# A first row map for the first two slots of a mixture of experts, and the whole map behind it

## The chip, the core and the metric

One core of a Trainium2 chip runs the whole program. The metric is device time in microseconds; of the kernel before there are three runs, 1336.71, 1337.16 and 1341.0, median 1337.16. Engines are named as the profile names them: PE is TensorE (PEld its weight loads), DVE VectorE, ACT ScalarE, POOL GpSimd, SP the engine that issues most DMAs.

## The reference, cut to what matters

The model adds four blocks to x (4 x 512 tokens, 256 features): a mixture of experts, a block-wise linear attention, a conditioned attention and a two-layer feed-forward stack with local attention. The change lies in the mixture of experts alone:

```python
gate = xn @ wg_W + wg_b + (genre_embed @ gg_W + gg_b)
gate_w = jax.nn.softmax(gate, axis=-1)
topk_w, topk_i = jax.lax.top_k(gate_w, 2)                 # 2 of 8 experts for each token
h1 = jax.nn.relu(jnp.einsum('bsh,ehm->bsem', x, W1) + b1) # 256 -> 512
h2 = jax.nn.relu(jnp.einsum('bsem,emn->bsen', h1, W2) + b2) # 512 -> 512
out_e = jnp.einsum('bsen,enh->bseh', h2, W3) + b3         # 512 -> 256
return jnp.einsum('bseh,bse->bsh', out_e, cw)
```

Only the two chosen experts count for a token, so the kernel sorts the 4096 (token, choice) pairs by expert and computes each pair once.

## The kernel before, in words

*Routing* (lines 1215 to 1445). TensorE transposes x and computes the gate logits; DVE finds the two best experts of each token (`eqs`); TensorE counts, with triangular matrices, how many earlier tokens chose the same expert (`ppos`, `pcnt`); some fifty short DVE instructions make of it a place in a list of expert slots (`slots`, 1391). `SLOTS` (41) is the order in which slots are worked: a first one of 128 places, then seven of 256, and so on. `eid` (1409) names the expert of each slot; it hangs only on the counts.

*The row map* (1412 to 1445). The kernel needs the inverse: which token stands at a place. A place number is split into its high part (place // 64) and low part (place % 64), `hl` (1399). For each group of four token tiles, DVE makes a one-hot of the low parts (`ol`, 1417: 64 columns for each of two choices) and of the high parts (`oh`, 1422: NHI = 80 columns); the low one is multiplied by the token number, for choice 0 by four ACT instructions (1426), for choice 1 by one of DVE (1427). TensorE sums the product of both over all 16 tiles in `pmap` (choice 0 in partitions 0 to 63, choice 1 in 64 to 127; 32 matmuls). `hmap` (1434) copies it, a matmul with `mfold` adds the halves (`pmap2`), and DVE makes `rowtok` (1439, 1440), the token to gather for each place, and `goal` (1442, 1445), the row to scatter its result to. Then `busy(4)` (1455) queues four matmuls of 128 x 512 whose result nobody reads.

*The slots* (1662 to 1726). `loads(j, d)` (1468) reads the slot's expert from `eid` into a register of SP and issues its weights: `w1` 516 KB, `w2` 1024 KB, `w3` 640 KB, two buffers of each. `fetch(j, d)` (1486) gathers the slot's tokens, 128 rows of 1 KB each, by an indirect DMA on POOL from `rowtok`. `turn_tokens` (1493) transposes them (`pxb`), and ACT copies them to `xbT`. `layer` makes `h1` and `h2` with `relu` (1457), whose instructions alternate between ACT and DVE; `last` makes the output rows, and `scatter` writes them. In the first slot the order on TensorE is: `pxb` of slot 0, first layer (8 matmuls), `pxb` of slot 1, second layer (16 matmuls), first layer of slot 1.

*What sets the order.* A scheduler orders each engine's queue, except what is `pinned` or lies in `PE.in_order()`, which keeps its place as written. Each engine works through its queue in order.

## Time and profile before

| | |
|---|---|
| median of three runs | 1337.16 us |
| the profiled execution's own time | 1343.32 us |
| its span, first to last instruction | 1341.6 us |
| mean granted TensorE clock | 0.983 |
| busy: PE, DVE, ACT, POOL | 95%, 51%, 43%, 22% |
| slots of the mixture of experts | about 46 to 290 us |

The profile is one execution. A row of a group or of the timeline gives start or count, engine, source line, operation and tiles, and in brackets what ended the idle time before it. `PEclk` is the share of the full clock that TensorE was granted. Most matmuls stand under line 82, a helper's line, so they are told apart by their tiles (`pmap`, `pxb`, `ph`). A matmul of this type shows as two records. Ends of matmuls are modelled.

### The profile page before, as it was taken

The page shows a single profiled execution, that of the slowest core. Times are in us where ns is not written, and L with a number is a line of the kernel's source. Part 1 is how long each engine was busy: PE and PEld are TensorE (multiplying, and loading weights), DVE is VectorE, ACT ScalarE, POOL GpSimd, SP SyncE. Part 2 cuts the span into 40 slices and gives each one's busy share as a digit, 9 for nine tenths or more (in the row PEclk, how much of TensorE's full clock was granted, in tenths as well). Part 3 has the DMA queues.
Part 4 walks back from the last instruction along what each step waited for, and adds up shares of the span by engine and source line. Part 5 has one row for each costly group of instructions (what it writes and reads, how often), then busy time and mean ns, then how long its engine had stood idle before and what let it go on. Part 6 is the DMA issues. An engine that isn't in the chain of part 4 may idle for free.

```text
span 1341.6 us, 23073 instructions
## 1 busy us (share of the span) xinstructions
PE 1271.8 (95%) x9214; PEld 812.2 (61%) x9214; DVE 683.4 (51%) x1464; ACT 581.4 (43%) x1157; POOL 292.9 (22%) x321
## 2 busy tenths in 40 slices
PE   4899999998999999999999999999999998999998
PEld 3788899964566634344344655766555556667654
DVE  6221243425777733242237788654372877864421
ACT  3221233326655365646644646561222655463111
POOL 1322356420000101010103334210030333422010
PEclk7899999998999999999999999999999999999999
DMA  3565666523000000000210001311001011012000
GB/s 96 213 236 192 236 239 221 189 76 116 1 1 1 1 1 1 0 1 1 91 57 14 18 18 27 104 34 25 24 0 43 25 30 30 18 43 56 18 21 22
DMA packets 41856, 85.29 MB, mean 64 GB/s; under 512 B 9409, under 2 KB 25673, under 8 KB 39433
## 3 DMA queue, kind: packets, MB, share of 16 engines
q1 hardware_dynamic: 36600, 73.02, 16.9%
q0 software_dynamic: 3504, 9.46, 2.1%
q8 instruction: 77, 1.26, 0.4%
q10 hardware_dynamic: 1632, 1.21, 0.3%
q14 instruction: 43, 0.34, 0.1%
HBM read 74.76 MB, written 6.82 MB: 61 GB/s over the span
## 4 chain that ended last, share of the span: by engine, by line
PE 75%; DVE 9%; DMA 6%; ACT 5%; issue 3%; POOL 1%; SPq 0%; DVEq 0%; POOLq 0%
PE ph L82 11%; PE pdq L82 7%; PE pfy L82 6%; PE sc L82 6%; PE pua L82 5%; PE pug L82 5%; PE pv L82 5%; PE pdy L82 4%; PE po L82 3%; PE pn L82 3%; DMA ys<-ob,goal 2%; PE pds L82 2%; PE pqk L82 1%; PE pz L82 1%; PE pqt L86 1%
## 5 line engine op out<-in xcount | busy, mean ns | idle before, releaser
L82 PE MATMUL pdq<-wqkv,yT 128*128 128x512 f32 x384 | 171.7, 597 | 2.4 <-DVE t L626 2.2
L424 ACT ACTIVATE cex<-sc 128x512 f32<-128x512 f32 x256 | 132.2, 604 | 85.6 <-PE sc L82 84.6
L82 PEld LDWEIGHTS pdq<-wqkv,yT 128*128 128x128 f32 x384 | 71.1, 190 | 84.6 <-issue 76.1
L82 PE MATMUL ph<-h,w 128*128 128x256 f32 (+2 forms) x576 | 121.5, 370 | 0.3 <-ACT h L1596 0.3
L629 POOL TENSOR_TENSOR qr<-t,t 128x512 f32<-128x512 f32 x64 | 81.3, 1271 | 140.5 <-DVE t L626 140.5
L82 PEld LDWEIGHTS ph<-h,w 128*128 128x128 f32 x576 | 102.0, 192 | 15.2 <-ACT h L1596 0.5
L1461 DVE TENSOR_SCALAR h<-ph,w 128x256 f32<-128x256 f32 (+2 forms) x52 | 23.0, 461 | 121.8 <-PE ph L82 101.7
L394 POOL TENSOR_SCALAR fterm<-vw,faT 128x256 f32<-128x256 f32 x16 | 14.6, 920 | 317.6 <-DVE cr L384 317.6
L82 PE MATMUL sc<-qm,kT 32*128 32x512 f32 x512 | 82.6, 639 | 0.0
L681 ACT ACTIVATE p<-pds,ss 128x192 f32<-128x192 f32 (+1 forms) x256 | 79.8, 425 | 2.1 <-PE pds L82 0.8
L82 PE MATMUL pua<-hT,w 128*128 128x512 f32 x160 | 75.3, 593 | 0.9 <-DVE z L706 0.9
L82 PE MATMUL pug<-hT,w 128*128 128x512 f32 x160 | 76.2, 598 | 0.0
L619 ACT ACTIVATE sq<-pdq 128x512 f32<-128x512 f32 x64 | 38.5, 601 | 83.7 <-POOL qr L629 42.2
L714 POOL TENSOR_TENSOR p<-p 128x192 f32<-128x192 f32 x64 | 42.4, 682 | 138.1 <-PE pn L82 135.3
L796 ACT ACTIVATE gl<-pug,cols 128x512 f32<-128x512 f32 x40 | 27.3, 687 | 93.6 <-PE pug L82 90.8
L82 PE MATMUL pv<-cex,v 128*32 128x512 f32 x512 | 61.9, 598 | 2.7 <-DVE vw L391 2.7
L82 PE MATMUL pfy<-w,uA 128*128 128x256 f32 x256 | 61.4, 383 | 0.0
L82 PE MATMUL po<-w,h 128*128 128x256 f32 x264 | 60.1, 380 | 0.0
L82 PE MATMUL pdy<-wo,oT 128*128 128x256 f32 x256 | 58.9, 383 | 0.0
L684 DVE TENSOR_TENSOR p<-p,lmask 128x384 f32<-128x384 f32 x64 | 47.0, 735 | 23.0 <-ACT p L681 21.6
L82 PE MATMUL pn<-p,v 64*64 64x128 f32 (+1 forms) x1792 | 50.3, 254 | 8.2 <-DVE p L687 4.2
L1459 ACT ACTIVATE h<-ph,w 128x256 f32<-128x256 f32 (+2 forms) x52 | 22.4, 455 | 81.9 <-PE ph L82 78.0
(352 smaller groups left out, 2329.8 us busy)
## 6 DMA issues: line engine op xcount, KB each, us to landing
w<-in_moe_w_dram SPq DMA_DIRECT2D x18, 1024.0 KB, 7.9
w<-in_moe_w_dram SPq DMA_DIRECT2D x18, 516.0 KB, 4.0
w<-in_moe_w_dram SPq DMA_DIRECT2D x14, 640.0 KB, 4.5
zb<-rows SPq DMA_DIRECT2D x32, 256.0 KB, 4.1
g<-ys SPq DMA_DIRECT2D x6, 512.0 KB, 6.9
wqkv<-in_f_wqkv_dram SPq DMA_DIRECT2D x2, 1536.0 KB
w<-in_f_w_dram SPq DMA_DIRECT2D x2, 1408.0 KB
w<-in_moe_w_dram SPq DMA_DIRECT2D x4, 512.0 KB
```

The costliest lines, as they stand in the source:

```text
L82: cls._queue(nc.tensor.matmul(*args, **kw))
L86: cls._queue(nc.tensor.transpose(*args, **kw))
L394: nc.gpsimd.tensor_scalar_mul(fterm[:, t, :], vw, W["faT"][:, t, b : b + 1])
L424: nc.scalar.activation(ex[:, i, :], pss[2 * j + i], AF.Exp, scale=CHD**-0.5)
L619: nc.scalar.activation(sq, p3, AF.Square)
L629: nc.gpsimd.tensor_tensor(qr_t[:, s], t1, t2, ALU.add)
L681: nc.scalar.activation(p[:, j * 192 : j * 192 + n], pss[j // 2][r][:, j % 2 * 192 : j % 2 * 192 + n], AF.Exp, scale=d.ss[:, j, 1, 2 * c + ...
L684: nc.vector.tensor_tensor(edges, edges, lmask[:, :128].rearrange("p (s q) -> p s q", q=64).unsqueeze(1).to_broadcast([128, 3, 2, 64]), ALU ...
L714: nc.gpsimd.tensor_tensor(p[:, 1:, 0:64], p[:, 1:, 0:64], p[:, : NT - 1, 128:], ALU.add)
L796: nc.scalar.activation(gl, pg, AF.Gelu, bias=col("bg", l * (NU + 1) + i))
L1459: pinned(nc.scalar.activation(dst, src, AF.Relu, bias=bias))
L1461: pinned(nc.vector.tensor_scalar(dst, src, bias, 0.0, ALU.add, ALU.max))
```

## The change

It makes two row maps in place of one. The first has only the three columns of places that the first two slots need (`first`: one of slot 0, two of slot 1). Its one-hots of the high parts are six columns wide, and they are multiplied by the token numbers instead of the low parts; the one-hots of the low parts are made in three long instructions for all 16 tiles and lie in buffers of the output (`ols`). A filler `busy(12)` is queued in front of it. The gathers of the first two slots read `early_rows`.

The whole map follows: `oh` by groups of four tiles, the low one-hots scaled in place, products of groups 0 to 2 with fillers `busy(2)` and `busy(1)` among them, the transposes of slot 0, and the products of group 3. Its copy precedes slot 0's first ReLU on DVE; its fold, `rowtok` and `goal` come behind slot 0's first layer. `busy(4)` is gone. Slots behind the first read their expert from `eids`, which has the values of `eid` and is computed from `early_rows` too, so that it is not there before it. In slot 0's second layer the transposes for slot 1 stand ahead of the last block of four matmuls; they stood ahead of the whole layer.

```diff
             PE.matmul(ppos[:, :128], tot, mtiles[:, :128], start=False, stop=True)
+            busy(12)
...
+            first = [2 * NPAIR + SLOTS[0][0], 2 * SLOTS[1][0], 2 * SLOTS[1][0] + 1]
+            oh0 = y[2].rearrange("p t h -> p (t h)")[:, : 12 * B * NT].rearrange("p (k i n) -> p k i n", k=2, n=6)
+            for at, r, n in ((0, first[0], 2), (2, first[1], 4)):
+                one_hot(oh0[:, :, :, at : at + n], hl[:, 0], miota[:, 2 * r : 2 * r + n])
+            tokens = mtok.rearrange("p (k i) -> p k i", k=2)
+            pinned(nc.vector.tensor_tensor(
+                oh0, oh0, tokens.unsqueeze(3).to_broadcast([128, 2, B * NT, 6]), ALU.mult))
+            ols = [y[k].rearrange("p t h -> p (t h)").rearrange("p (i n) -> p i n", n=64) for k in (1, 3)]
+            one_hot(ols[0], hl[:, 1, 0], miota[:, :64])
+            for i0 in (0, B * NT // 2):
+                one_hot(ols[1][:, i0 : i0 + B * NT // 2], hl[:, 1, 1, i0 : i0 + B * NT // 2], miota[:, :64])
...
+            def map_products(pmap, n, onehot, k, tiles):
+                for i in tiles:
+                    PE.matmul(pmap[64 * k : 64 * k + 64, : 2 * n], ols[k][:, i, :], onehot(k, i),
+                              start=(i == 0), stop=(i == B * NT - 1))
...
+            with PE.in_order():
+                pmap = acct("pmap")
+                for k in range(2):
+                    map_products(pmap, 3, lambda k, i: oh0[:, k, i, :], k, range(B * NT))
+                early_rows = map_rows(map_copied(pmap, 3), 3)[1]
+            xbs = [hp.tile([128, 2, H], F32, tag="xb", name="xb", bufs=3) for j in range(2)]
+            gather(xbs[0][:, 0, :], early_rows, 0)
+            for i in range(2):
+                gather(xbs[1][:, i, :], early_rows, 1 + i)
...
+            eids = xp.tile([128, 1], I32, tag="eids", name="eids")
+            pinned(nc.vector.scalar_tensor_tensor(eids, early_rows[:, 0:1], 0.0, eid, ALU.min, ALU.max))
...
+            for g in range(4):
+                full_onehots(g)
+            busy(2)
+            for g in range(3):
+                full_products(g)
+                if g == 0:
+                    busy(1)
...
-                e = nc.sync.value_load(eid[j : j + 1, 0:1], min_val=0, max_val=NE - 1)
+                e = nc.sync.value_load((eids if j else eid)[j : j + 1, 0:1], min_val=0, max_val=NE - 1)
...
-            fetch(0, ds[0])
-            fetch(1, ds[1])
+            ds[0].xb, ds[1].xb = xbs
             with PE.in_order():
                 turn_tokens(ds[0])
+                full_products(3)
+            with PE.in_order():
+                full_map = map_copied(pmap, NROWT)
...
                         h1 = layer(d, d.xbT, "h1", w1, 0)
+                    if j == 0:
+                        rowtok, goal = full_rows()
...
-                    d.h2 = layer(d, h1, "h2", d.w2, 4)
+                    d.h2 = layer(d, h1, "h2", d.w2, 4, None if j else lambda: turn_tokens(after))
```

`full_onehots(g)` makes `oh` for four tiles (128 x 640) and scales four tiles of `ols` in place: choice 0 by four ACT instructions, choice 1 by one of DVE. `full_products(g)` is eight matmuls. `map_copied`, `map_rows` and `full_rows` are the old lines 1433 to 1445, now with a width.

More of the change, by code (lines that the diff above doesn't have):

```diff
@@ L1323, in adaln_attn_ffn_kernel, with busy @@
             PE.matmul(ppos[:, :128], tot, mtiles[:, :128], start=False, stop=True)
+            def busy(n):
+                with PE.in_order():
+                    ps = mmt("pbusy")
+                    for _ in range(n):
+                        PE.matmul(ps, ident, xres[0].rearrange("p t h -> p (t h)")[:, :512], start=True, stop=True)
+            busy(12)
             E2 = [128, NE, 3 * NE]
@@ L1399, in adaln_attn_ffn_kernel, with one_hot @@
             nc.vector.tensor_copy(hl, hli)
+            def one_hot(out, of, iota):
+                shape = list(of.shape) + [iota.shape[1]]
+                for _ in of.shape[1:]:
+                    iota = iota.unsqueeze(1)
+                tc.keep_in_program_order(nc.vector.tensor_tensor(
+                    out, of.unsqueeze(len(of.shape)).to_broadcast(shape), iota.to_broadcast(shape), ALU.is_equal))
+            first = [2 * NPAIR + SLOTS[0][0], 2 * SLOTS[1][0], 2 * SLOTS[1][0] + 1]
+            oh0 = y[2].rearrange("p t h -> p (t h)")[:, : 12 * B * NT].rearrange("p (k i n) -> p k i n", k=2, n=6)
@@ new lines, in adaln_attn_ffn_kernel, with map_copied @@
+            for i0 in (0, B * NT // 2):
[4 more added lines that the diff above has]
+                              start=(i == 0), stop=(i == B * NT - 1))
+            def map_copied(pmap, n):
+                half_map = xp.tile([128, n, 2], F32, tag=f"hmap{n}", name="hmap")
+                pinned(nc.vector.tensor_copy(half_map, pmap[:, : 2 * n].rearrange("p (r q) -> p r q", q=2)))
+                return half_map
@@ new lines, in map_rows @@
+            def map_rows(half_map, n):
+                pmap2 = acct("pmap2")
+                for q in range(2):
+                    PE.matmul(pmap2[64 * q : 64 * q + 64, :n], mfold, half_map[:, :, q], start=True, stop=True)
+                rowtok = xp.tile([128, n], I32, tag=f"rowtok{n}", name="rowtok")
+                pinned(nc.vector.tensor_scalar(rowtok, pmap2[:, :n], -1.0, 0.0, ALU.add, ALU.max))
+                pinned(nc.vector.tensor_single_scalar(rowtok, rowtok, B * S - 1, op=ALU.bitwise_and))
+                return pmap2, rowtok
@@ new lines, in gather @@
+            def gather(dst, table, r):
+                pinned(nc.gpsimd.indirect_dma_start(
+                    out=dst, out_offset=None, in_=xall,
+                    in_offset=bass.IndirectOffsetOnAxis(ap=table[:, r : r + 1], axis=0)))
+            with PE.in_order():
[3 more added lines that the diff above has]
+                early_rows = map_rows(map_copied(pmap, 3), 3)[1]
@@ L1411, in adaln_attn_ffn_kernel @@
             nc.vector.tensor_copy(nhalf, halfs[0:1, NE - 1 : NE])
+            eids = xp.tile([128, 1], I32, tag="eids", name="eids")
+            pinned(nc.vector.scalar_tensor_tensor(eids, early_rows[:, 0:1], 0.0, eid, ALU.min, ALU.max))
             pmap = acct("pmap")
-            for i0 in range(0, B * NT, 4):
-                i1 = i0 + 4
-                O4 = [128, 2, 4, 64]
-                ol = hp.tile(O4, F32, tag="ob", name="ol", bufs=3)
-                nc.vector.tensor_tensor(
-                    ol, hl[:, 1, :, i0:i1].unsqueeze(3).to_broadcast(O4),
-                    miota[:, :64].unsqueeze(1).unsqueeze(1).to_broadcast(O4), ALU.is_equal)
-                H4 = [128, 2, 4, NHI]
-                oh = hp.tile(H4, F32, tag="h1", name="oh")
-                nc.vector.tensor_tensor(
-                    oh, hl[:, 0, :, i0:i1].unsqueeze(3).to_broadcast(H4),
-                    miota.unsqueeze(1).unsqueeze(1).to_broadcast(H4), ALU.is_equal)
-                for i in range(i0, i1):
-                    nc.scalar.mul(ol[:, 0, i - i0, :], ol[:, 0, i - i0, :], mtok[:, i : i + 1])
-                nc.vector.tensor_tensor(
-                    ol[:, 1], ol[:, 1], mtok[:, B * NT + i0 : B * NT + i1].unsqueeze(2).to_broadcast([128, 4, 64]), ALU.mult)
-                for i in range(i0, i1):
-                    for k in range(2):
-                        PE.matmul(pmap[64 * k : 64 * k + 64, :NHI], ol[:, k, i - i0, :], oh[:, k, i - i0, :],
-                                  start=(i == 0), stop=(i == B * NT - 1))
@@ L1433, in adaln_attn_ffn_kernel @@
-            half_map = xp.tile([128, NROWT, 2], F32, tag="hmap", name="hmap")
-            nc.vector.tensor_copy(half_map, pmap[:, :NHI].rearrange("p (r q) -> p r q", q=2))
-            pmap2 = acct("pmap2")
-            for q in range(2):
-                PE.matmul(pmap2[64 * q : 64 * q + 64, :NROWT], mfold, half_map[:, :, q], start=True, stop=True)
-            rowtok = xp.tile([128, NROWT], I32, tag="rowtok", name="rowtok")
-            nc.vector.tensor_scalar(rowtok, pmap2[:, :NROWT], -1.0, 0.0, ALU.add, ALU.max)
@@ L1440, in adaln_attn_ffn_kernel @@
-            nc.vector.tensor_single_scalar(rowtok, rowtok, B * S - 1, op=ALU.bitwise_and)
-            goalf = xp.tile([128, NROWT], F32, tag="goalf", name="goalf")
-            nc.vector.scalar_tensor_tensor(goalf, pmap2[:, :NROWT], 0.0, maside.to_broadcast([128, NROWT]),
-                                           ALU.is_equal, ALU.mult)
-            goal = xp.tile([128, NROWT], I32, tag="goal", name="goal")
-            nc.vector.tensor_tensor(goal, pmap2[:, :NROWT], goalf, ALU.add)
-            def busy(n):
-                with PE.in_order():
-                    ps = mmt("pbusy")
-                    for _ in range(n):
-                        PE.matmul(ps, ident, xres[0].rearrange("p t h -> p (t h)")[:, :512], start=True, stop=True)
@@ L1455, in adaln_attn_ffn_kernel, with full_onehots @@
-            busy(4)
+            ohs = []
+            def full_onehots(g):
+                tiles = slice(4 * g, 4 * g + 4)
+                oh = hp.tile([128, 2, 4, NHI], F32, tag=f"h{1 + g // 2}", name="oh")
+                one_hot(oh, hl[:, 0, :, tiles], miota)
+                for i in range(4 * g, 4 * g + 4):
+                    pinned(nc.scalar.mul(ols[0][:, i, :], ols[0][:, i, :], mtok[:, i : i + 1]))
+                pinned(nc.vector.tensor_tensor(
+                    ols[1][:, tiles], ols[1][:, tiles], tokens[:, 1, tiles].unsqueeze(2).to_broadcast([128, 4, 64]),
+                    ALU.mult))
+                ohs.append(oh)
@@ new lines, in full_products, with full_rows @@
+            def full_products(g):
+                with PE.in_order():
+                    for i in range(4 * g, 4 * g + 4):
+                        for k in range(2):
+                            map_products(pmap, NROWT, lambda k, i: ohs[i // 4][:, k, i % 4, :], k, [i])
+            for g in range(4):
[5 more added lines that the diff above has]
+                    busy(1)
+            def full_rows():
+                pmap2, rowtok = map_rows(full_map, NROWT)
+                goalf = xp.tile([128, NROWT], F32, tag="goalf", name="goalf")
+                pinned(nc.vector.scalar_tensor_tensor(
+                    goalf, pmap2[:, :NROWT], 0.0, maside.to_broadcast([128, NROWT]), ALU.is_equal, ALU.mult))
+                goal = xp.tile([128, NROWT], I32, tag="goal", name="goal")
+                pinned(nc.vector.tensor_tensor(goal, pmap2[:, :NROWT], goalf, ALU.add))
+                return rowtok, goal
@@ L1489, in fetch @@
                     r = place(d.n, SLOTS[j][0]) + i
-                    pinned(nc.gpsimd.indirect_dma_start(
-                        out=d.xb[:, i, :], out_offset=None, in_=xall,
-                        in_offset=bass.IndirectOffsetOnAxis(ap=rowtok[:, r : r + 1], axis=0)))
+                    gather(d.xb[:, i, :], rowtok, r)
             def turn_tokens(d):
@@ L1521, in wide_layer, with layer @@
                 return dst
-            def layer(d, src, tag, w, bias):
+            def layer(d, src, tag, w, bias, between=None):
                 if d.wide:
@@ L1534, in layer @@
                            [(w[:, c, m * 128 : (m + 1) * 128], src[:, c, 0:n]) for c in range(w.shape[1])])
+                        if between is not None and m == 2:
+                            between()
                     if d.n == 2:
@@ L1670, in adaln_attn_ffn_kernel @@
             loads(0, ds[0])
-            fetch(0, ds[0])
-            fetch(1, ds[1])
+            ds[0].xb, ds[1].xb = xbs
             with PE.in_order():
                 turn_tokens(ds[0])
+                full_products(3)
+            with PE.in_order():
+                full_map = map_copied(pmap, NROWT)
             last_wide = max(j for j, d in enumerate(ds) if d.wide)
@@ L1704, in adaln_attn_ffn_kernel @@
                     if j == 0:
-                        pinned(nc.gpsimd.indirect_dma_start(
-                            out=xtail, out_offset=None, in_=xall,
-                            in_offset=bass.IndirectOffsetOnAxis(ap=rowtok[:, TAILS : TAILS + 1], axis=0)))
+                        gather(xtail, rowtok, TAILS)
                     if j == last_wide + 3:
@@ L1719, in adaln_attn_ffn_kernel @@
                             xres[j - 10], xres[j - 10], row("bo").unsqueeze(1).to_broadcast([128, NT, H]), ALU.add))
-                    if j + 1 < len(often):
+                    if 0 < j < len(often) - 1:
                         turn_tokens(after)
-                    d.h2 = layer(d, h1, "h2", d.w2, 4)
+                    d.h2 = layer(d, h1, "h2", d.w2, 4, None if j else lambda: turn_tokens(after))
                     if d.wide:
```

## The prediction

> **What bounds the kernel now.** The page first: TensorE is busy for 95% of the span and makes 75% of the chain that ended last. A change to routing can only help where TensorE waits or runs slowly. So I read the chain from the end of the position arithmetic to the second slot:

> ```profile
> 30.57 0.69 DVE ol L1417
> ...
> 38.21 0.25 DVE hmap L1434
> ...
> 38.87 0.20 DVE rowtok L1439
> ...
> 39.58 5.59 DMA xb<-in_x_dram,rowtok
> 45.17 0.04 issue
> 45.21 0.45 PE pxb L86 x2
> 45.69 0.38 ACT xbT L1503
> 46.07 0.04 issue
> 46.11 2.66 PE ph L82 x16
> ```

> Columns: start, duration (us), what. From `hl` (30.5) to the first layer (46.1) are 15.6 us in which TensorE does nothing that later slots need; 5.59 of them are the first gather. Behind 46.11 TensorE is nearly gapless for slots of 15 us, so what the start of the first layer gains is kept to the end.

> Next the clock, in the stretches between which it switches (columns: TensorE busy, weight loads, DVE, ACT, POOL, granted clock, DMA share, GB/s):

> ```profile
> 20.07:30.31 10.24, 2.17 (x8) 1.86 (x8) 8.98 (x58) 0.45 (x2) 0.00 (x0) 0.50 0.00 1
> 30.31:33.73 3.42, 1.57 (x16) 1.36 (x16) 3.35 (x7) 1.82 (x8) 0.00 (x0) 0.50 0.78 241
> 33.73:37.14 3.41, 3.14 (x32) 2.72 (x33) 3.41 (x7) 2.13 (x10) 0.00 (x0) 0.50 1.00 411
> 37.14:40.55 3.41, 3.05 (x24) 1.86 (x25) 0.99 (x6) 0.30 (x2) 0.97 (x1) 1.00 1.03 426
> 40.55:43.96 3.41, 1.91 (x5) 0.57 (x3) 0.00 (x0) 0.00 (x0) 2.50 (x4) 1.00 0.82 317
> 43.96:47.38 3.42, 1.71 (x13) 1.47 (x14) 0.00 (x0) 0.37 (x1) 2.32 (x3) 1.00 0.38 115
> 47.38:50.79 3.41, 3.41 (x19) 3.40 (x18) 0.70 (x2) 1.21 (x3) 0.00 (x0) 0.50 0.14 38
> ```

> The clock goes in steps of 3.41 us: half through the whole map, full after the stretch filled to 3.14, half again after one filled to 1.71, which falls into the first slot. DMA runs at 411 to 426 GB/s while the map is made: both slots' weights, which the gather has to pass.

> Last, the rows that price the new steps:

> ```profile
> 11.64 0.96 PEld L82 LDWEIGHTS pgb<-ggw,csB 64*128 64x128 f32 x8 [0.17 <-DVE gb L1243]
> ...
> 31.18 0.82 DVE L1422 TENSOR_TENSOR oh<-hl,mc 128x640 f32<-128x640 f32 x1
> ...
> 38.76 3.70 PE L82 MATMUL pbusy<-xres,ident 128*128 128x512 f32 x8
> ```

> A matmul in this type is two passes (busy(4) shows x8), and a busy pass of 512 columns takes 0.43 us at full clock. Eight loads of 128 columns with next to nothing to multiply start 0.11 us apart ((0.96-0.19)/7).

> **The change, step by step,** with this execution's clock steps.

> *The filler busy(12)* stands in TensorE's queue ahead of the first map. It starts when `ppos` ends, about 23.6. Up to the step at 26.9 its passes take 0.86: 3.3 us, 3.9 passes. The other 20.1 x 0.43 = 8.6, so it ends at 35.5.

> *First one-hots.* By the rows of 128x512 (0.69) and 128x640 (0.82) an element costs 1.0 ns above some 0.16 us. The small pieces (64, 128 and 192 elements) make 0.8 us, the 1024-element one 1.2, the two of 512 0.6 each back to back: the first half is ready at 32.6, all at 33.8. So they cost nothing, but only because the filler covers them to 35.5; without it the products could start at 32.6. The filler is 2.9 us too long for this trace, and I count that.

> *First map's products.* 32 matmuls, 64 passes, loads of 64 columns, 6 columns to multiply. [...] The `pgb` row shows that the load sets the pace: half of 0.11 is 0.056 us, so 3.6 us. The products of one half of the array now come in a row, so loads of the two halves don't overlap as in the old map. I take the row: done at 39.1, `hmap` at 39.3. [...] The old map had `hmap` at 38.21, so this step is 1.1 us later than before.

> *Copy, fold, rowtok, gather.* Was 38.21 to 39.58 = 1.37. With 6 and 3 columns in place of 80 and 40, and no `goalf` between, I take 0.2 off: gather at 40.5.

> *The gather.* The second slot's loads now read `eids`, which waits for the first row map. Issued at 40.2, `eids` lands some 0.15 later; from `eid` (28.95) to the first load was 1.03, so those weights are issued at 41.4. Until then the queue holds 2.18 MB, which at 411 GB/s takes 5.3 us from 31 and is through before the gather. The median of 33 gathers is 3.3 us, the shortest 2.7, the longest 6.1. I take 3.3 (nearest: the later gathers), landing at 43.8 instead of 45.17; bounds 2.7 and 5.6. Behind the wait on SP are the second slot's three loads and 13 more register loads (0.57 each, 7.4 us): SP is free for slot 2 at 50.5, when the old trace issued those at 55.53. The second slot's first weights land at about 45, wanted at 52. Its two gathers follow on POOL by 1.3 us each and share DMA with its weights until about 48; wanted at 51.

> *The whole map in the hole.* DVE starts at 40.3: four groups of one-hot and scaling, 0.73 + 0.34 (spacing of 31.18, 31.91, 32.25) = 1.07, the last at 44.65. ACT's 16 scalings (4.2 us) wait for the first half's products and end at 41.5. TensorE: busy(2) to 41.6, group 0 to 42.15 (16 passes, 0.55 as in the old last group), busy(1) to 43.0, groups 1 and 2 to 44.2, transposes to 44.65, group 3 to 45.2. `xbT` is ready at 45.1. First layer at 45.2 against 46.11: -0.9. DVE's chain ends last here, not the gather.

> *First slot.* Was 46.11 to 53.54 = 7.4. Now at full clock: 16 passes of 0.112 and their drain 2.05, four ReLUs 0.4 apart (48.81, 49.21, 49.60, 50.00) that end 1.55 later, the rest of the first block 0.2, two blocks 1.8, the next tokens' transposes 0.45, the last block 0.9: 7.0. The second fold (4 passes) hides in the ReLU wait where the transposes were; those now cost their 0.45. The 1.7 us of half clock come to only 0.45 because the ReLUs already hid most of them. Full rowtok and goal come after the second ReLU on DVE, some 49.4; slot 2's gathers issued there land at 54, wanted at 57.

> Sum: -0.9 - 0.45 = -1.4. On this execution (span 1341.6, 1343.3 with 1.7 around it) that is 1341.9. It lies 6.2 above the median of the runs, perhaps in part from half-clock stretches later (303 to 314 shows 0.53) that the change doesn't touch. So I apply it to the median: 1337.2 - 1.4 = **1335.8**.

> **Rivals.**

> *The clock closes in the new map (slower).* [...] The rows say more: a stretch filled to 1.71 of 3.42 was enough, one of 1.91 was not. Products of 6 columns may count as little. The stretch 33.73 to 37.14 then holds 1.8 us of filler, right between the two. If it closes there, 35 passes take twice as long (+1.9), all behind shifts, some is won back from DVE's slack: first layer at 48.0, +1.9 - 0.45 = +1.4, 1338.6. It decides from 1.4 us of lost time. For it: 1.71 closed. Against: weight loads run without a gap. If it closes only at 40.55, the fillers and groups run at half and the layer starts at 46.4: -0.2, 1337.0. [...]

> *The gather gains nothing.* The second slot's weights are issued 0.9 us after it, where its data start about 1.7 us after issue. If it takes 5.6 again: landing 46.1, layer at 47.0, +0.45, 1337.6. For it: one gather took 6.1. Against: it is ahead in the queues.

> [...]

> **Chances.** Forecast 0.48 (own range 1334.7 to 1337), closing in the map 0.17, closing behind it 0.12, gather as before 0.12, floor 0.06, rest 0.05 (an unseen stall). The measurement can tell about 0.3% (4 us); no case reaches it alone, but the three runs span 4.3, so I leave 0.12 below 1333.2 and 0.13 above 1341.2. Range for 8 in 10: 1333.0, just below the floor case, to 1340.0, both slower cases together with half a microsecond.

> **What would show it.** Right: the last `pbusy` of the first filler ends near 35.5, the first map's loads are 0.056 apart, `xb` lands 3.3 after issue, clock 1.00 from 27 to 54, first layer near 45.2, second near 52.2. Wrong: a clock of 0.50 between 37 and 51, the first gather above 5, a wait of the second slot for `w` or `xb`, or any difference behind the second slot.

## Result and the profile after

| | before | after |
|---|---|---|
| median of nine runs each | 1341.0 us (1336.71 to 1345.94) | 1346.29 us (1344.24 to 1351.31) |
| profiled execution, its span | 1343.32, 1341.6 us | 1345.46, 1343.7 us |

The ratio of the runs is 1.0046, with a 95% interval of 1.0031 to 1.0061. A later set (22 and 28 runs, the first experiment) gives 1.0036 (1.0026 to 1.0046). So the change costs 4 to 6 us. The three runs from which I forecast lay low: in the later sets, each beside other kernels, the kernel before has a median of 1339.9 to 1340.9.

First the chain of the kernel after, through routing (start, us, what):

```profile
36.69 3.64 PE pmap L82 x64
40.32 0.02 issue
40.34 0.18 DVE hmap L1435
...
41.54 5.51 DMA xb<-in_x_dram,rowtok
47.06 0.04 issue
47.10 0.44 PE pxb L86 x2
47.54 0.70 PE pmap L82 x16
48.24 2.00 PE ph L82 x16
```

Before, the gather stood in this chain from 39.58 with 5.59 us, and the first layer began at 46.11; now the gather starts 2 us later, takes as long, and the layer begins at 48.17. The first slot gains some of it back (7.1 us to the second slot's first layer in place of 7.5): that one begins at 55.29 against 53.65.

That +1.6 explains less than half. I matched the matmuls of both traces and followed the shift between them. In the pair of profiled executions it is +1.7 at 55 us, -2.0 at 755 (the half-clock stretch that begins at 303 is shorter after, that of 692 is absent), +4.4 at 935, and +2.0 at the end (the half clock at 1132 of the trace before is absent after). Single executions scatter so; the loss of 4 to 6 us is that of all runs. The rise from -2.0 to +4.4 lies where the change doesn't reach: in the attention stage from 795 to 935 us. There DVE waits for DMAs that turn rows in DRAM (`zb`, for the softmax's sums) or between partitions (`hn`). The waits of this stretch, first before, then after (engine, line waited for: us in total, times, longest):

```profile
DVE oT L739 <- DMA zb<-rows: 9.0, 5, 2.7
DVE st L762 <- DMA hn<-yc: 3.3, 3, 1.9
```

```profile
DVE oT L739 <- DMA zb<-rows: 12.8, 5, 3.6
DVE st L762 <- DMA hn<-yc: 6.5, 3, 3.4
```

Together 12.3 us have become 19.3. The first of these waits, in the timeline before and after, in brackets the idle time and its releaser:

```profile
808.34 0.49 DVE L762 BATCH_NORM_STATS2 st<-hn 128x6 f32<-128x128 f32 x2 [0.34 <-DMA hn<-yc]
```

```profile
808.07 0.49 DVE L762 BATCH_NORM_STATS2 st<-hn 128x6 f32<-128x128 f32 x2 [1.99 <-DMA hn<-yc]
```

What moved in between? The DMA view, over the stretch from the first `hn` issue to that instruction (queues with packets, MB, share; issues with KB and us to landing), before and after:

```profile
q1 hardware_dynamic: 545, 0.26, 21.7%
q14 instruction: 1, 0.01, 0.6%
...
hn<-yc SPq DMA_DIRECT2D x1, 30.0 KB, 2.4
```

```profile
q1 hardware_dynamic: 553, 0.27, 17.2%
q8 instruction: 1, 0.02, 1.4%
q14 instruction: 1, 0.01, 0.5%
...
hn<-yc SPq DMA_DIRECT2D x1, 30.0 KB, 4.0
```

A packet of the queue `q8 instruction` has come into the middle of the transfer, and it lands after 4.0 us in place of 2.4. This packet has 16 KB and is under way for 1.50 us (804.62 to 806.12); in the kernel before the neighbouring ones come at 799.7 and 809.1, one before the transfer and one behind it. There are 77 of them in both kernels, in the kernel before for 18,757 records of TensorE (9214 weight loads, as many passes, 329 of its sequencer), one in 244. From one packet to the next TensorE starts 255 records in the median, 257 in the changed kernel. So I took these packets for TensorE's program, 256 instructions in each; the padding below agrees: 256 further instructions bring one packet more, the 78th, and leave the transfer free of it, 180 put one into it. The change lengthens it: 45 further matmuls (11 of filler, 32 of the first map, 2 of its fold) of four instructions each (two passes, a load for each), 180; the trace has 181 records more (one is the sequencer's). From there to the end each block begins some 180 instructions earlier in the work: by the count of records, the packet of the same number comes only 4 later in the median.

What the fetch does to the transfer can be counted. Of its 508 pieces of 512 bytes (224 and 30 KB) nearly all have started by 806.0, as fast as before; 32 of them, one sixteenth, start later, one by one until 807.4, most when the fetch is through. With 45 padding matmuls (below) it is 32 again. The profile's page counts 16 DMA engines.

That gave the theory: **the place of the fetches costs some 3 us far behind the change, the routing stage itself some 2.**

### The profile page after: what moved, and what is told of

Its sections match the earlier page's. It is cut to its first block, busy times and chain, and to the rows that moved or that the text cites. A ratio compares the mean times of both kernels' runs of the same rounds, so it can differ in the third digit from the quotient of the medians.

```text
span 1343.7 us, 23271 instructions
## 1 busy us (share of the span) xinstructions
PE 1283.0 (95%) x9304; PEld 815.2 (61%) x9304; DVE 684.8 (51%) x1470; ACT 581.0 (43%) x1157; POOL 293.1 (22%) x321
## 3 DMA queue, kind: packets, MB, share of 16 engines
q10 hardware_dynamic: 1632, 1.21, 0.3%
## 4 chain that ended last, share of the span: by engine, by line
PE 72%; DVE 10%; DMA 9%; ACT 5%; issue 3%; POOL 1%; SPq 0%; DVEq 0%; POOLq 0%
PE ph L82 11%; PE pdq L82 6%; PE sc L82 6%; PE pfy L82 5%; PE pua L82 5%; PE pv L82 5%; PE pug L82 5%; PE pdy L82 4%; PE po L82 3%; DMA ys<-ob,goal 2%; DMA zb<-rows 2%; PE pn L82 2%; PE pqk L82 1%; PE pqt L86 1%; DVE t L626 1%
## 5 line engine op out<-in xcount | busy, mean ns | idle before, releaser
L82 PE MATMUL pdq<-wqkv,yT 128*128 128x512 f32 x384 | 171.7, 597 | 2.7 <-DVE t L626 2.4
L82 PEld LDWEIGHTS pdq<-wqkv,yT 128*128 128x128 f32 x384 | 71.1, 190 | 84.7 <-issue 76.0
L82 PE MATMUL ph<-h,w 128*128 128x256 f32 (+2 forms) x576 | 121.6, 369 | 0.5 <-ACT h L1651 0.3
L82 PEld LDWEIGHTS ph<-h,w 128*128 128x128 f32 x576 | 101.5, 191 | 15.8 <-ACT h L1651 0.5
L82 PE MATMUL sc<-qm,kT 32*128 32x512 f32 x512 | 82.5, 639 | 0.0
L82 PE MATMUL pua<-hT,w 128*128 128x512 f32 x160 | 76.8, 603 | 2.5 <-DVE z L706 2.5
L82 PE MATMUL pug<-hT,w 128*128 128x512 f32 x160 | 76.4, 600 | 0.0
L714 POOL TENSOR_TENSOR p<-p 128x192 f32<-128x192 f32 x64 | 41.4, 667 | 139.0 <-PE pn L82 136.1
L82 PE MATMUL pv<-cex,v 128*32 128x512 f32 x512 | 61.9, 598 | 2.7 <-DVE vw L391 2.7
L82 PE MATMUL pfy<-w,uA 128*128 128x256 f32 x256 | 61.4, 383 | 0.0
L82 PE MATMUL po<-w,h 128*128 128x256 f32 x264 | 60.1, 380 | 0.0
L82 PE MATMUL pdy<-wo,oT 128*128 128x256 f32 x256 | 59.5, 384 | 0.3 <-DVE oT L739 0.3
L684 DVE TENSOR_TENSOR p<-p,lmask 128x384 f32<-128x384 f32 x64 | 47.1, 736 | 23.3 <-ACT p L681 22.0
L797 DVE SCALAR_TENSOR_TENSOR uA<-pua,cols,gl 128x512 f32<-128x512 f32 x32 | 23.8, 749 | 65.7 <-PE pua L82 56.1
L82 PE MATMUL pn<-p,v 64*64 64x128 f32 (+1 forms) x1792 | 49.9, 252 | 7.2 <-DVE p L687 3.5
```

Source lines behind the costliest of these rows:

```text
L82: cls._queue(nc.tensor.matmul(*args, **kw))
L684: nc.vector.tensor_tensor(edges, edges, lmask[:, :128].rearrange("p (s q) -> p s q", q=64).unsqueeze(1).to_broadcast([128, 3, 2, 64]), ALU ...
L714: nc.gpsimd.tensor_tensor(p[:, 1:, 0:64], p[:, 1:, 0:64], p[:, : NT - 1, 128:], ALU.add)
L797: nc.vector.scalar_tensor_tensor(f.u[i // 4][:, i % 4, :], pa, col("ba", l * (NU + 1) + i), gl, ALU.add, ALU.mult)
```

## Experiments

The ratio is always to the kernel before, run on the same chip, with its 95% interval; one thousandth is 1.34 us.

### Mending the routing stage

`late`: the second slot's weights are issued behind the one-hots of the whole map, so that no transfer meets the first gather. `filler8`: the filler is as long as the one-hots need.

```diff
+            eids_late = xp.tile([128, 1], I32, tag="eids2", name="eids_late")     # late
+            pinned(nc.vector.scalar_tensor_tensor(eids_late, early_rows[:, 0:1], 0.0, eids, ALU.min, ALU.max))
...
-                e = nc.sync.value_load((eids if j else eid)[j : j + 1, 0:1], min_val=0, max_val=NE - 1)
+                e = nc.sync.value_load((eids_late if j else eid)[j : j + 1, 0:1], min_val=0, max_val=NE - 1)
...
-            busy(12)
+            busy(8)                                                               # filler8
```

The change once more:

> The changed kernel once more, beside the three versions that follow, so that all stand on one chip; its second trace also shows what of the first was chance. Theory (the routing stage loses some 1.5 us: a filler that ends 2.5 us behind the ready one-hots, and a gather that is met by the second slot's weights): first map's products from about 36.5, first gather 5.5 us after its issue again, first layer near 48.2, second slot near 55.2, and a total that lies 1 to 2 us above the kernel before, the rest of the measured 6 us being the place of half-clock windows. Rival (something behind the second slot costs the larger part every time): the shift against the kernel before grows from +1.4 at slot 2 to +4 or more by the end in this trace too, at the same instructions as in the first trace; total again +5 to +6.

> The second slot's weights are issued some 5 us later (their expert number is copied once more behind the four groups of one-hots on VectorE), so no transfer meets the first gather. Nothing else moves. Theory: the gather lands about 3.3 us after its issue (44.8 in place of 47.1), the scaled one-hots of the last group (45.7) then end last, first layer near 46.3 (-1.9), total -2 against the changed kernel, if the second slot's weights (issued near 47, landing near 52) don't come late for it at 53. [...]

> The filler ahead of the first map has 8 matmuls in place of 12 (16 passes, so about 3.4 us less at full clock). Theory: the first map's products start when the last one-hot is ready or soon behind the filler, near 33.3 to 34 in place of 36.6; everything up to the first layer comes 2.6 to 3 us earlier; the gather still takes 5.5; first layer near 45.5, total -2.7 against the changed kernel, some 1 to 2 us under the kernel before. Rival (the clock needs the whole filler): the clock falls to half in or behind the first map, its 64 passes take 7.2 us in place of 3.6, first layer at 48 or later, total the same or slower. Second rival: the step from half to full comes with the phase of the 3.41 us windows, so that a shorter filler doesn't open it at all before the products.

> Both edits. Theory: first map's products from 33.3 to 34, gather issued near 38.8 and landed near 42, the last group of one-hots near 43, first layer near 43.5 (-4.6 against the changed kernel, -2.6 against the kernel before), total -4.5 against the changed kernel. If the loss sits behind the second slot instead, the first layer moves so, but the total stays above the kernel before by 2 us or more.

| | first map from | first layer from | shift at 755, 935, end | ratio |
|---|---|---|---|---|
| change again | 36.62 | 47.90 | -1.2, +1.1, +1.2 | 1.0036 (1.0026 to 1.0046) |
| late | 35.22 | 47.03 | -0.3, +4.7, +4.7 | 1.0037 (1.0017 to 1.0057) |
| filler8 | 33.05 | 46.19 | -0.5, +4.3, +6.3 | 1.0049 (1.0033 to 1.0065) |
| both | 33.12 | 44.89 | -3.8, -1.0, -1.9 | 1.0033 (1.002 to 1.0046) |

The first layer came earlier by 1 to 3 us, though each time less than expected, and the total did not follow: my theory of that moment, that routing was the loss, fell, and the rival (a loss behind it) held in the totals. In the trace of the change again it held in part: the shift grew at the same place, but by 2.3 us, and ended at +1.2 instead of +4. All five traces of the change's family grow by 2.3 to 6.4 us between 755 and 935, and in all the fetch near 804 to 807 lies in the `hn` transfer.

### Moving the fetches alone

Matmuls of 8 x 1 that nobody reads make TensorE's program longer and change nothing else. In the kernel before they stand behind `ppos`, where TensorE idles for 8.4 us (23.8 to 32.15), 45 of them (180 instructions, as in the change) or 64 (256, a whole block):

```diff
+            def pads(n):
+                with PE.in_order():
+                    ps = mmt("pads")
+                    for _ in range(n):
+                        PE.matmul(ps[:8, :1], ident[:, :8], ident[:, :1], start=True, stop=True)
+
+            pads(45)        # control: pads(64)
```

> The kernel before with 45 matmuls of 8x1 that nobody reads, queued on TensorE where it idles from 23.8 to 31 us. Nothing of the routing change is in it: the padding only makes TensorE's program longer by as many instructions (180 weight loads and passes) as the change does. Theory (the time behind the second slot is lost because the 16 KB pieces in which TensorE's instructions are fetched by DMA, one per 256 instructions, now fall on other places, and in places delay a small DMA that DVE and TensorE wait for): the fetches behind 740 us stand as in the changed kernel (one about 3 us after the last normalised rows near 802, where the kernel before has them before and behind), the wait for hn there is 2.0 in place of 0.34, and the total is 2 to 4 us above the kernel before. Rival (the loss comes with the changed tiles, queues or clock of routing): the total stays within 1 us of the kernel before.

> The control: 64 such matmuls in place of 45, 256 instructions, a whole fetch. Theory: the fetches behind the padding stand where they stood in the kernel before, one piece later in number; the wait for hn near 808 is 0.3 again, and the total is that of the kernel before within 1 us, up to what the padding itself costs if it doesn't fit into the idle 7 us (seen at the first layer's start). Rival (more instructions cost, wherever they fall): slower than with 45.

Measured: 45 give 1.0027 (1.0015 to 1.0038), 64 give 0.9989 (0.9978 to 1.0001), which is 1.5 us under where 1 at most was expected, with equality just inside the interval. More instructions cost less than fewer, though the first layer starts alike in both (46.57 and 46.55). The same DMA view for 45 and for 64:

```profile
q8 instruction: 1, 0.02, 1.6%
...
hn<-yc SPq DMA_DIRECT2D x1, 30.0 KB, 4.1
```

```profile
q1 hardware_dynamic: 545, 0.26, 21.2%
q14 instruction: 1, 0.01, 0.4%
...
hn<-yc SPq DMA_DIRECT2D x1, 30.0 KB, 2.3
```

With 180 instructions the kernel before has a fetch in the transfer like the changed kernel's, a landing after 4.1 us and a wait of 2.10; with 256 it has its own 2.3 and 0.32 again. The other engines' programs have as many records as before in both. So the place of the fetches by itself costs 3.6 us (2.0 to 5.1). The profiled execution with 45 isn't typical: it is the slowest of its 14, and a half-clock stretch in the first slot (45.2 to 52.1) put its second slot 1.4 late. Over all runs the clock can account for little: the mean granted clock is 0.9846 with 45 and 0.9853 before, which by estimate is 0.9 us at most (0.0007 of 1340). How the fetch delays the transfer is not shown: one sixteenth of the pieces comes late, but the trace doesn't say which of the 16 DMA engines a packet used.

### Putting the fetches back in the change

The same `pads`, so that change and padding make 256 instructions. With a filler of 8 (which takes 16 away) these are 23:

> The changed kernel with a filler of 8 in place of 12 matmuls and 23 of 8x1 in front of it: 180 - 16 + 92 = 256 instructions more than the kernel before. The routing stage is about that of the changed kernel or of the filler-8 version (first layer 46 to 48). Theory: fetches as in the kernel before, hn wait near 808 0.3, and a total of the kernel before plus what the first layer loses, 0 to +1.5 us: 3 to 4 us under the filler-8 version without padding. Rival: the same as that version, +6.

> The same padding with both mends of the routing stage (filler of 8; the second slot's weights issued after the first gather has landed). Theory: both losses are gone: first layer near 44 to 45, fetches as in the kernel before, total 0.5 to 2 us under the kernel before, 4 to 5 us under the same version without padding. Rival: as that version without padding, +4.

> The changed kernel as it is, with 19 matmuls of 8x1 that nobody reads ahead of its filler: 180 + 76 = 256 instructions more than the kernel before, so the fetches of TensorE's program stand as there. The padding delays filler and first map by some 0.5 us. Theory: what is left of the loss is the routing stage's own: first layer near 48.5 (gather 5.5 after its issue), shift at the third slot +1.5 to +2, waits for zb and hn between 795 and 960 us together 12 to 13 us as in the kernel before (15.7 to 19.3 in the kernels with other places of the fetches), total +1.5 to +2 against the kernel before. Rival: total +5.

Measured: filler 8 goes from 1.0049 to 1.0005 (0.9994 to 1.0016), both mends from 1.0033 to 0.9986 (0.9975 to 0.9997): 6 us each, for 23 idle matmuls more. Against the kernel before, both are as expected; the difference that the padding makes is larger than expected (3 to 5). The third, the change with its own filler, missed: 1.0034 (1.0021 to 1.0047), where +1.5 to +2 us was expected. Its fetches were right (the waits for `hn` 3.3 us in all, growth between 755 and 935 only 1.3), but its second slot began 5.8 late: the padding had delayed the first map to 37.58, and half clock fell on 39.9 to 46.7. So the padding was put where it delays nothing, ahead of `ptot`, with TensorE waiting for `pick`:

```diff
+            with PE.in_order():
+                ps = mmt("pads")
+                for _ in range(19):
+                    PE.matmul(ps[:8, :1], ident[:, :8], ident[:, :1], start=True, stop=True)
             ptot = mmt("ptot")
```

> The changed kernel with the 19 padding matmuls in an earlier hole (17 to 21.6 us, where TensorE waits for the chosen experts), so that the 256 further instructions are there, but neither filler nor first map is delayed. In the run with the padding ahead of the filler the first map came 1 us later and a half-clock stretch of 6.8 us (39.9 to 46.7) fell behind it, so its +4.6 doesn't tell the fetches' share. Theory (three terms: place of the fetches 2.6 to 6, second slot's weights meeting the gather 1.3, and half-clock windows that close in or behind the first map, 1.6 each): first map from about 36.6, and if the clock stays open as in the two traces of the changed kernel, shift of +1.3 to +1.7 at the third slot and about that at the end; total 1 to 3 above the kernel before, 2 to 4 under the changed kernel without padding. If the clock closes, shift +3 to +5. Rival (the fetches explain only the padding experiments on the kernel before): +4.5 or more with the clock open.

> Filler of 8, the second slot's weights after the first gather, and 23 padding matmuls in the earlier hole (256 further instructions in all). Against the version with the padding ahead of the filler, the first map starts near 33.2 in place of 34.8. Theory: first layer near 43.4 with the clock open (first map's start + 10.2), near 45 if one half-clock window falls behind it; total 1 to 3 us under the kernel before. Rival (shorter filler closes the clock at once): first layer at 45 or later, total as with the padding ahead.

Measured: the change with 19 early ones 1.0016 (1.0004 to 1.0028), which is +2.1 us (0.5 to 3.8), with a shift of +1.4 at the third slot: the routing stage's own loss. Total and shift are as expected for an open clock, but in this trace the clock closed (40.2 to 43.6), for which +3 to +5 had been expected; the first map also started 1.0 earlier than expected (35.59), so the two offset each other by chance. Against the 1.0036 without padding the fetches make 2.7 us of the change's loss; against 1.0046, 4.0. These are differences between sets on different chips; by the intervals they may be off by 2.1 and 2.6. Both mends with 23 early ones give 0.9987 (0.9973 to 1.0001), first layer at 44.50. The two paddings of the mended kernel thus lie 1.5 to 2 us under the kernel before; the interval of the first excludes equality, that of the second just includes it.

### Was the place before a lucky one?

Both mends with 31, 39 and 55 padding matmuls, which puts the fetches 32, 64 and 128 instructions further on than in the kernel before:

> Both mends of routing (filler of 8, late weights of the second slot) with 31 padding matmuls: the fetches 32 instructions further on than in the kernel before. Is the kernel before's place a lucky one? Theory: total and waits depend on the place: at this one, near the kernel before's, the waits between 795 and 960 us are within 2 us of 12.5, total within 1.5 of the version with 23. First layer near 45.3.

> As before with 39 padding matmuls: fetches 64 instructions further on. Theory: the waits between 795 and 960 us and the total come out at some place between the kernel before's (12.5) and the changed kernel's (16 to 19); which, the theory can't say. First layer near 45.5. If it is faster than with 23, the kernel before's place was no optimum.

> As before with 55 padding matmuls: fetches half a piece (128 instructions) further on. Theory: again between or beyond the two known places, with the total following the waits for zb and hn between 795 and 960 us (1 us of wait is about 1 us of total, and a half-clock window near 875 more where the wait is long). First layer near 46. Rival (only the place of the kernel before is good by chance of its tuning): waits of 15 or more at 64 and at 128.

Measured: 1.0007 (0.9993 to 1.0022), 1.0000 (0.9989 to 1.0011) and 1.0057 (1.0044 to 1.007). All runs together, by how far the fetches stand from those of the kernel before ("wait": `zb` and `hn` from 795 to 960; "growth": of the shift from 755 to 935):

| instructions further, modulo 256 | kernels | wait | growth |
|---|---|---|---|
| 0 | before; six with padding to 256 | 12.0 to 14.1 | 0 to 2.0 (mean of the six 1.0) |
| 32, 64 | both mends | 13.4, 12.6 | 1.6, 1.4 |
| 128 | both mends | 14.7 | 3.7 |
| 164, 180 | the change twice, late, filler8, both, before with 45 | 15.7 to 19.3 | 2.3 to 6.5 (mean 4.6) |

No padding lost more than the one at 128, but that one also had two half-clock stretches behind its first map (second slot +3.1). By waits and growth, the places from 0 to 64 are about as good as the kernel before's, and from 128 to 180 they are worse; the rest wasn't tried. The rival (waits of 15 or more at 64 and at 128) did not hold. In the totals 32 and 64 lie 2.8 and 1.9 us above the same kernel at 0 (0.9986), where 32 was expected within 1.5; some 1 us of it is there at the second slot already (shift -0.3 and -0.7 in place of -1.4), and the rest is about what the intervals leave open.

The first wait for `hn`, near 808, tells the places apart in all 16 traces: in seven a fetch falls into the transfer and the wait is 1.65 to 2.10 us (the six of the last row and 128); in the other nine none does and it is 0.31 to 0.36. In four of the six traces of the last row, and in none of the others, a wait near 873 is followed by a half-clock stretch (it begins between 875 and 878), which adds some 3 us: those four have grown by 4.7 or more, the other two by 2.3 and 2.8.

### What the routing stage costs

All traces with the new map, by two questions: do the second slot's weights meet the gather, and does half clock fall between first map and first layer? Time from the start of the first map to the first layer:

| | clock full | one stretch of 3.41 at half | two |
|---|---|---|---|
| weights meet the gather | 11.3, 11.6 | 12.3 | 13.1, 13.6, 14.7 |
| weights late | 10.2, 10.2 | 11.7, 11.8, 11.8, 11.8 | 13.2 |

Late weights are worth 1.2 us with the clock full, and a stretch at half then costs 1.5; where the weights meet the gather, one costs 0.8 in the one trace that has it. With late weights and full clock the chain looks like this (filler 8 and late, 23 padding matmuls ahead of the filler):

```profile
34.89 3.63 PE pmap L82 x64
...
42.73 1.26 PE pmap L82 x32
43.98 0.44 PE pxb L86 x2
44.42 0.70 PE pmap L82 x16
45.12 2.00 PE ph L82 x16
```

The gather has left the chain (issued at 39.75, used at 43.98: 4.2); fillers and products carry it. And why half clock? The clock changes in steps of 3.41 us (the changed kernel's first switches: 8.18, 18.42, 28.66, 3 of them apart), called windows here. The windows around the products of the first map, first of `late`, then of the changed kernel (columns as in the prediction):

```profile
36.18:39.59 3.41, 3.15 (x56) 3.05 (x55) 0.26 (x2) 3.30 (x14) 0.00 (x0) 1.00 0.30 124
39.59:43.01 3.42, 3.42 (x6) 0.89 (x7) 3.35 (x9) 0.00 (x0) 2.56 (x2) 0.50 0.11 37
```

```profile
35.49:38.90 3.41, 3.41 (x46) 2.48 (x44) 0.00 (x0) 1.97 (x9) 0.00 (x0) 1.00 0.52 216
38.90:42.31 3.41, 3.15 (x33) 2.19 (x31) 1.51 (x6) 1.96 (x9) 0.77 (x1) 1.00 0.00 0
```

In `late` a whole window holds little but products of 6 columns: TensorE counts as busy for 3.15 of 3.41 us, and the next window is at half all the same. In the changed kernel the window takes in the end of the filler (its last 1.1 us), and the next stays full. But no rule follows from this contrast: with 19 padding matmuls ahead of its filler the changed kernel fills a window alike, again with 1.1 us of filler, and the next is at half:

```profile
36.48:39.89 3.41, 3.41 (x46) 2.50 (x45) 0.00 (x0) 2.00 (x9) 0.00 (x0) 1.00 0.12 51
39.89:43.30 3.41, 3.15 (x29) 3.05 (x29) 0.44 (x3) 1.93 (x9) 0.00 (x0) 0.50 0.00 0
```

In all traces that lose the clock here, the half follows the window with the most products of the first map. Where these fill 2.31 us of it or more, it follows in 7 of 7 traces; at 1.87 to 2.28, in 2 of 6. What decides in between stays open. Where the windows lie differs between executions that are alike up to there: the clock opens at 28.66 in the changed kernel and at 25.94 in `late`. So the rival that the clock closes in or behind the new map has no plain yes or no: it happened in 9 of 13 traces with this map, in neither of the changed kernel's own two. I didn't widen the products to test it.

## Why the prediction was wrong

Sign and size were wrong: 1335.8 forecast, -1.4 against the kernel before, and 4 to 6 us more than the kernel before measured. Of the 10.5 us between 1335.8 and 1346.29, 3.8 are the low median of the three first runs. The rest, by the prediction's steps:

- **The filler ends at 35.5.** It ended at 36.6. The clock opened at 28.66, not 26.9, since the windows lay otherwise in that execution: 1 us of the sum. "2.9 us too long" was right in kind: with 8 the map started 3.5 us earlier.
- **One-hots ready at 33.8.** 33.98. Right.
- **First map's products, 3.6 by the row.** 3.64, spaced 0.055 on average. Right: the row's pace held. No run shows the floor to which the prediction gave a chance of 0.06 and by which it set the lower end of its range; the runs show this spacing in its place.
- **Copy to gather.** From `hmap` to the gather 1.2, as said.
- **The gather takes 3.3.** 5.51, as before: the named rival. I had the second slot's weights 0.9 us behind it in the queue and took that for enough. They came 0.7 behind and overtook it: between 41.5 and 45.0 us 103 packets of weights moved and none of the gather. Its data began 3.5 us after its issue; the 1.7 that I used were those of a later gather, and the first one of the trace before had taken 2.6. In the five traces in which TensorE waits for a gather with these weights behind it, it takes 5.3 to 7.6 us; with the weights late, 4.2 in the one trace in which something waits for it. This term was short by 2.2 us, of which the weights make 1.3 by that one trace.
- **DVE's four groups of 1.07, chain of DVE last.** 1.07 each; ready at 45.74 as against 44.65, since they began 1.1 later; but the gather ended last, at 47.1.
- **The first slot takes 7.0 in place of 7.4.** 7.1 against 7.5. Right.
- **"Behind 46.11 TensorE is nearly gapless ..., so what the start of the first layer gains is kept to the end."** This is the step that failed, and it made about half of that rest. The shift isn't kept: between 755 and 935 it grew by 6.4 and 2.3 us in the two traces of the change, and over all runs the fetches cost 2.7 to 4.0, because 45 further matmuls moved all later fetches of TensorE's program. I had priced them at their time on the engine only, and had looked for waits in the slots alone, though the trace before has 12.3 us of waits for `zb` and `hn` between 795 and 960. The text listed "any difference behind the second slot" as a sign of error, but gave it no price.

The sum in the terms that the runs support: routing +2.1 (0.5 to 3.8; +1.6 and +1.4 in the second slot of its two traces), place of the fetches +2.7 to +4.0. How much of the second term is half clock behind the waits and how much the longer waits themselves differs: the mean granted clock gives the half clock at most 0.9 of 3.6 us for the 45 matmuls, and nothing of the 6 us that the padding is worth with both mends (0.9890 without and with 23). For filler 8 (0.9858 and 0.9877) it may by the same estimate be 2.5 of 6. What remains open: how the fetch delays the transfer, and which padding is best; the differences among the good ones are about as large as the intervals.

## What to carry to other kernels

## What the runs showed of the hardware that I had not expected

- With one packet of 16 KB of TensorE's program among its pieces of 512 bytes (under way for 1.50 us; 0.9 to 1.8 for all packets of the kernels before and after) a transfer landed after 4.0 in place of 2.4 us, and DVE waited for it 1.99 in place of 0.34. TensorE itself works on without a gap from 804.57 to 807.2, while this fetch of the changed kernel is under way; here another transfer pays.
- Being busy didn't by itself keep TensorE's clock: in `late` half clock followed a window with 3.15 of 3.41 us busy, nearly all of it passes with 6 columns and their loads (3.05 us of loading).
- 128 passes of 8 x 1 took 3.35 us (0.026 each) at half clock, by the 0.78 us of `ppos` just before them, the same as in the kernel before at 0.50; and 45 such matmuls in an idle hole moved the total by 3.6 us.
